# Two-layer attention and FFN kernel: another order of loads and work at the start, gathers tied to chunks, and a written order at the end

## The chip, the cores and the metric

The kernel runs on one core of a Trainium2 chip. The engines are named as the profile names them: PE is TensorE (matmuls and transposes), DVE is VectorE, ACT is ScalarE, POOL is GpSimd, SP is SyncE, which only starts transfers. PEld is PE's loading of weights. The metric is the device time of one execution in microseconds (us); lower is better. Three runs of the kernel before gave 328.57 us in the median, from 328.22 to 328.8.

## The reference

`x` is 2 batches of 1024 rows of 256 numbers, the context is 2 batches of 77 rows of 192. All is float32. Four stages follow one another, each with a residual:

```python
x = x + L0_xattn(layernorm(x), ctx)    # 16 heads of 16, softmax over the 77 context rows
x = x + L0_ffn(layernorm(x))           # relu FFN 256 -> 1024 -> 256; only expert 0 counts; then a layernorm
x = x + L1_xattn(layernorm(x), ctx)    # one head of 256, its own layernorms of x and of the context
x = x + L1_ffn(layernorm(x))           # each position takes one of 8 matrices of 256x256 and one of 8 biases

# L1_ffn
scores = einsum('sp,tp->st', pe, sign(tile_sigs))   # 1024 positions, 8 tiles
idx = argmax(scores, axis=-1)                       # the same for both batches
y_all = einsum('bsd,tod->bsto', x, W) + b
out = take y_all at idx
```

The choice of a matrix depends on the position alone, not on `x`.

## The kernel before

The 2048 rows are cut into 8 chunks of 256 (`NC`), each of two blocks of 128 rows (`NI`); chunks 0 to 3 are batch 0, chunks 4 to 7 batch 1. A chunk goes through `attention0` (with one `attention0_block` per block), `ffn0`, `attention1` and `to_pairs`. All are generators: each `yield` names a place in an abstract order, `begin` puts a generator on a heap, and `run` takes them from the heap by place. So the stages of several chunks are woven into each other: `attention0` of chunk c near place 2c - 2, `ffn0` near 2c + 2.7, `attention1` near 2c + 6. A scheduler below places the instructions on the engines; inside `tc.manual_schedule` an engine keeps the order in which the program wrote them.

For the last stage the 1024 positions are sorted by matrix. `choices` computes scores, the chosen matrix (`oh`), and by counting and triangular sums each row's place in the sorted order (`to`) and its inverse (`who`). Rows of batch 0 are computed in their given order and sent to their sorted places through a DRAM tensor `places` (`to_places`, `from_places`); rows of batch 1 are gathered in sorted order from the start (`rows_of_x`). A sorted batch has 8 blocks of 128 rows; a block can span several matrices, and 15 pairs of a block and a matrix (`NJ`) always cover it. `pairs` computes which block and which matrix each pair has and loads these numbers into registers of ACT, PE and DVE. `pair` copies a block's transposed rows (`nT`, ACT), multiplies them by its matrix (`ps_t`, PE, four matmuls in the trace) and adds the result, scaled by `scale`, to the block's rows `y` (DVE). `scale` is zero for rows that are not the pair's, and otherwise the row's inverse standard deviation. From pair 7 on each pair finishes one block, which POOL scatters to its rows of `out`: eight indirect transfers for each batch.

Because the registers hide which block a pair touches, the program tells the framework which dependences do not hold: `apart` and `apart_of` call `declare_no_dep`. For the scatters, "no row is written twice" takes away the order between them.

Row statistics come from `moments`: two DVE instructions per block, then the inverse root, usually on POOL (an addition and a power). `inverse_root` does it on DVE with twelve small instructions for the second norm of `ffn0` in chunks 6 and 7, and for both later norms of chunk 7.

`beginning` writes the order at the start: six warming matmuls, then `choices`' first step, the context, the keys and chunk 0's rows. The loads stand in front of it. SP starts x of chunk 0, `cols` (all constant columns), `wq`, `wv`, x of chunk 1, `wo`, `rows`; ACT starts the context, `wk`, `sigT` and `peT`. Loads after `late = True` wait until chunk 0's normalised rows have been transposed and copied (`after(loads.pop(), "a0")`).

`PLACES` gives the pairs' places: batch 0 from 18.7 to 21.05, batch 1 from 21.05 to 23.7. Batch 0's pairs so lie between the last chunk's instructions. Gathers keep program order on POOL (`keep_in_program_order`).

Of the kernel before, what the change touches and what calls it, by code (L numbers as in the profile page):

```python
# [37 lines left out]
P = 128  # L38
# [25 lines left out]
def tile_blocks(ctx: ExitStack, tc: tile.TileContext, a: dict, out: bass.AP):  # L64
# [50 lines left out]
    cols = load("cols", [P, N_COL], a["cols"])  # L115
    wq = load("wq", [P, KC, D], rows_of(a["wq"]))
    sigT = load("sigT", [P, NT], a["sigT"], nc.scalar)
    peT = load("peT", [P, S // 4], a["peT"], nc.scalar, tag="hT", bufs=6)
    wv = load_early(1, "wv", CK)
    load_x(1)  # L120
    wo = load("wo", [P, KC, D], rows_of(a["wo"]))

    rows = load("rows", [P, N_ROW, D], a["rows"].partition_broadcast(P))
    late = True
    w1 = load("w1", [P, KC, F], rows_of(a["w1"][0]), tag="w1", bufs=1)
    load_x(2)
    wk1 = load_early(2, "wk1", CK)
# [61 lines left out]
    def moments(x, n, name, p=P, twice=False, vector=False, rs=None, later=False, pin=False):  # L189
        st = work.tile([P, NI, nc.vector.BN_STATS_DIM], F32, tag="st", name=f"st_{name}")  # L190
        mv = work.tile([P, NI, nc.vector.BN_AGGR_DIM], F32, tag="mv", name=f"mv_{name}", bufs=6)
        if rs is None:
            rs = work.tile([P, NI], F32, tag="rs", name=f"rs_{name}", bufs=6)
        for i in range(n):
            ins = nc.vector.bn_stats(st[:p, i, :], x[:p, i, :])  # L195
            if pin:
                tc.keep_in_program_order(ins)
        for i in range(n):
            nc.vector.bn_aggr(mv[:p, i, :], st[:p, i, :])


        eps = EPS * EPS / (1.0 + EPS) if twice else EPS

        def root():
            if vector:
                inverse_root(rs, mv[:, :, 1], eps, name)
            else:
                nc.gpsimd.tensor_scalar(rs[:p, :n], mv[:p, :n, 1], eps, None, ALU.add)
                nc.gpsimd.tensor_tensor(rs[:p, :n], rs[:p, :n], mhalf[:p, :n], ALU.pow)

        if later:
            return mv, rs, root
        root()
        return mv, rs

    def inverse_root(y, v, eps, name):
        w = work.tile([P, NI], F32, tag="w", name=f"w_{name}")
        t = work.tile([P, NI], F32, tag="t", name=f"t_{name}")  # L220
        nc.vector.tensor_scalar(w, v, eps, None, ALU.add)
        yi = y.bitcast(I32)
        nc.vector.tensor_scalar(yi, w.bitcast(I32), 1, None, ALU.logical_shift_right)
        nc.vector.tensor_scalar(yi, yi, -1.0, float(0x5F3759DF), ALU.mult, ALU.add)
        for _ in range(3):
            nc.vector.scalar_tensor_tensor(t, y, -0.5, y, ALU.mult, ALU.mult)
            nc.vector.tensor_tensor(t, t, w, ALU.mult)
            nc.vector.scalar_tensor_tensor(y, t, 1.5, y, ALU.add, ALU.mult)

    def normed(x, n, d, name, m, p=P, out=None, act=False):  # L230
# [10 lines left out]
        for i in range(n):  # L241
            if act:
# [12 lines left out]
    def centred(x, name, mv, act):  # L255
        y = work.tile([P, NI, D], F32, tag="xn", name=f"n_{name}", bufs=4)
        if act:
            sh = work.tile([P, NI], F32, tag="sh", name=f"sh_{name}", bufs=4)
            nc.vector.tensor_scalar(sh, mv[:, :, 0], -1.0, None, ALU.mult)
        for i in range(NI):  # L260
            if act:
                nc.scalar.activation(y[:, i, :], x[:, i, :], AF.Identity, bias=sh[:, i : i + 1])
            else:
                nc.vector.tensor_scalar(y[:, i, :], x[:, i, :], mv[:, i, 0:1], None, ALU.subtract)
# [90 lines left out]
    def masked(e, c, src, eng):  # L355
        mask = cols[:, C_VM + 8 * c : C_VM + 8 * c + 8].unsqueeze(1).unsqueeze(3)
        eng.tensor_tensor(
# [5 lines left out]
    def values():  # L363
# [9 lines left out]
        for c in range(NK):  # L373
# [6 lines left out]
            masked(0, c, ps[:, :D], nc.vector)  # L380
# [8 lines left out]
    def values_by_head():  # L389
        y = work.tile([P, NK, D], F32, tag="ext", name="ext", bufs=1)  # L390
        nc.sync.dma_start(y, v_rows.rearrange("(c p) d -> p c d", p=P))
        for c in range(NK):
            yield
            masked(1, c, y[:, c, :], nc.gpsimd)


    def row_of_biases():
        bvb = work.tile([P, KC, P], F32, tag="oT", name="bvb")
        for k in range(KC):
            nc.vector.tensor_scalar(bvb[:, k, :], ones, col(C_BV + k), None, ALU.mult)  # L400
# [9 lines left out]
    def second_context():  # L410
        m = moments(cx, B, "cx", p=L)
# [62 lines left out]
    def choices():  # L474
        neg = const.tile([P, NT], F32, tag="neg", name="neg")
        sign = const.tile([P, NT], F32, tag="sign", name="sign")
        nc.vector.tensor_scalar(neg, sigT, 0.0, None, ALU.is_lt)
# [156 lines left out]
    def gather(to, src, index):  # L634
        tc.keep_in_program_order(
            nc.gpsimd.indirect_dma_start(
                out=to, out_offset=None, in_=src,
                in_offset=bass.IndirectOffsetOnAxis(ap=index, axis=0),
            )
        )  # L640

    def rows_of_x(c):
        e, s0 = divmod(c * NI, NS)
        for i in range(NI):
            gather(
                xs[c][:, i, :], a["x"].rearrange("b s d -> (b s) d"),
                chosen["who"][:, e, s0 + i : s0 + i + 1],
# [7 lines left out]
    def attention0(c, x):  # L655
        e = c * NI // NS
        m = moments(x, NI, f"a{c}", pin=1 < c < 4)
        yield 2 * c - 1.8
        n = normed(x, NI, D, f"a{c}", m, act=True)
# [11 lines left out]
        for g in range(KC):  # L671
            nc.scalar.activation(qT[:, g, :], ps[:, g, :], AF.Identity, bias=col(C_BQ + g))  # L672
# [72 lines left out]

    def ffn0(c, x):
# [10 lines left out]
        for f in range(0, F // P, 2):  # L757
# [9 lines left out]
            for j in range(2):  # L767
                nc.scalar.activation(  # L768
                    hT[-1][:, j, :], ps[:, j, :], AF.Relu, bias=col(C_B1 + f + j)
                )  # L770
        for i in range(NI):
# [9 lines left out]
        m = moments(tb, NI, f"g{c}", vector=c >= NC - 2)  # L781
# [11 lines left out]
    def attention1(c, x, b):  # L793
        e = c * NI // NS
        keys = slice(e * L, (e + 1) * L)
        last = c == NC - 1
        mv, rs, root = moments(x, NI, f"b{c}", twice=True, vector=last, later=True)
        if not last:
            root()
        yield b + 6.3  # L800
        n = centred(x, f"b{c}", mv, act=not last)
        if last:
            root()
# [49 lines left out]

    def apart(i, others, reason):
        for other in others:
            tc.declare_no_dep(i.ins, other, reason=reason)
# [21 lines left out]
    def apart_of(ins, others, reason):  # L878
        for other in others:
# [258 lines left out]
```

## Time and profile before

The profiled execution took 331.53 us, its span from the first to the last instruction is 329.8 us, and the granted clock of PE was 0.964 in the mean.

| engine | busy us | share of the span | instructions |
|---|---|---|---|
| PE | 289.5 | 88% | 2100 |
| PEld | 241.0 | 73% | 2100 |
| DVE | 206.0 | 62% | 604 |
| ACT | 152.0 | 46% | 331 |
| POOL | 121.5 | 37% | 167 |

The whole span in 40 slices of 8.2 us each, a digit being tenths of busy time (9 is 90% or more), and the clock that PE was granted:

```profile
PE   3997929999969999899899999999995989987690
DVE  1538844947837775594768459468477575675740
PEclk9999987999999999999999999999997899999788
```

In a table by stage, the columns are the stretch in us, its length, the busy time of PE, PEld, DVE, ACT and POOL (with the number of instructions), PE's granted clock, the share of the DMA engines and GB/s. In a row of the order of time, the columns are the start in us, the duration, the engine, the line, the operation, what it writes and reads, and in brackets the idle time before it with what ended it. In a row of the chain of waits they are the start, the time on the chain, and what took it.

### The profile page before, as it was taken

To read this page: it belongs to the slowest core of one execution; us is meant where nothing else is said; L and a number is where in the kernel's file an instruction comes from. 1 tells how busy PE (TensorE), PEld (TensorE's weight loads), DVE (VectorE), ACT (ScalarE), POOL (GpSimd) and SP (SyncE) were. 2 spreads that over 40 slices of the span, in tenths; PEclk is the share of its full clock that TensorE was granted. 3 is DMA by queue.
4 is the path that set the end of the run, shared out by engine and by line. 5 is a ranking of instruction groups with operands and counts; after the bars stand their busy time and mean duration, and the time that the engine had idled before them with its cause. 6 is when DMAs were issued, how large, how long until landed. Compare 5 with 4: busy or idle time off the path is not lost.

```text
span 329.8 us, 5754 instructions
## 1 busy us (share of the span) xinstructions
PE 289.5 (88%) x2100; PEld 241.0 (73%) x2100; DVE 206.0 (62%) x604; ACT 152.0 (46%) x331; POOL 121.5 (37%) x167
## 2 busy tenths in 40 slices
PE   3997929999969999899899999999995989987690
PEld 3865718878858887788688788888885878865470
DVE  1538844947837775594768459468477575675740
ACT  1234427465365455547444663645554464242210
POOL 2210372223271455515454451123175530173153
PEclk9999987999999999999999999999997899999788
DMA  8394210330010001100200100040000000011011
GB/s 221 104 359 134 81 32 0 114 143 3 2 46 4 17 14 43 40 2 17 66 17 5 46 17 2 0 159 2 3 1 0 2 0 0 0 68 64 0 67 64
DMA packets 10456, 16.13 MB, mean 49 GB/s; under 512 B 1186, under 2 KB 7740, under 8 KB 10428
## 3 DMA queue, kind: packets, MB, share of 16 engines
q1 hardware_dynamic: 7847, 10.06, 9.4%
q0 software_dynamic: 1920, 5.25, 5.3%
q10 hardware_dynamic: 661, 0.45, 0.6%
q8 instruction: 17, 0.28, 0.3%
q14 instruction: 11, 0.09, 0.1%
HBM read 11.95 MB, written 3.80 MB: 48 GB/s over the span
## 4 chain that ended last, share of the span: by engine, by line
PE 63%; DVE 18%; POOL 6%; ACT 4%; issue 3%; DMA 3%; DVEq 1%; POOLq 0%; ACTq 0%
PE ps_h L763 14%; PE ps_eo L775 12%; PE ps_t L936 5%; PE ps_pT L721 5%; PE sc L686 4%; PE ps_y L743 3%; PE ps_o L730 3%; PE ps_s L812 3%; PE ps_q L667 3%; DVE pr L697 2%; DVE sm L704 2%; DVE y L941 2%; PE ps_y L838 2%; DMA sigT<-in_sigT 2%; DVE x L789 1%
## 5 line engine op out<-in xcount | busy, mean ns | idle before, releaser
L763 PE MATMUL ps_h<-xT_f,w 128*128 128x256 f32 x256 | 62.3, 386 | 0.2
L775 PE MATMUL ps_eo<-w,hT 128*128 128x256 f32 x256 | 60.4, 391 | 0.0
L775 PEld LDWEIGHTS ps_eo<-w,hT 128*128 128x128 f32 x256 | 49.2, 197 | 6.6 <-DVE st_a L195 0.2
L763 PEld LDWEIGHTS ps_h<-xT_f,w 128*128 128x128 f32 x256 | 46.8, 190 | 8.8 <-issue 2.0
L701 ACT ACTIVATE pr<-pr 128x616 f32<-128x616 f32 x32 | 22.9, 717 | 43.3 <-DVE pr L697 40.3
L695 DVE TENSOR_REDUCE mx<-sc 128x8 f32<-128x616 f32 x32 | 25.2, 788 | 13.4 <-PE sc L686 13.4
L936 PE MATMUL ps_t<-every,nT 128*128 x120 | 31.0, 410 | 2.6 <-DVE y L941 1.3
L768 ACT ACTIVATE hT<-ps_h,cols 128x256 f32<-128x256 f32 x64 | 26.6, 467 | 10.7 <-PE ps_h L763 10.4
L936 PEld LDWEIGHTS ps_t<-every,nT 128*128 128x128 f32 x120 | 24.0, 207 | 7.3 <-ACT nT L930 2.7
L722 ACT COPY pT<-ps_pT 128x512 f32<-128x512 f32 x48 | 25.4, 594 | 5.0 <-PE ps_pT L721 4.9
L653 POOL TENSOR_TENSOR x<-x,rows 128x512 f32<-128x512 f32 x16 | 20.4, 1280 | 19.0 <-DVE rows L404 16.7
L704 DVE TENSOR_REDUCE sm<-pr 128x8 f32<-128x616 f32 x32 | 25.2, 786 | 3.4 <-ACT pr L701 2.5
L743 PE MATMUL ps_y<-wo,oT 128*128 128x256 f32 x64 | 17.9, 404 | 9.3 <-DVE oT L737 9.3
L721 PE MATMUL ps_pT<-ident,pr 128*128 128x128 f32 x160 | 21.4, 279 | 4.7 <-ACT qT L672 2.7
L697 DVE TENSOR_TENSOR pr<-sc,mx 128x616 f32<-128x616 f32 x32 | 25.3, 790 | 0.2
L721 PEld LDWEIGHTS ps_pT<-ident,pr 128*128 128x128 f32 x160 | 18.7, 145 | 6.6 <-ACT qT L672 2.9
L941 DVE SCALAR_TENSOR_TENSOR y<-ps_t,scale,y 128x256 f32 x30 | 14.4, 479 | 11.5 <-PE ps_t L936 8.7
L947 POOL DMA_INDIRECT out<-y,who x16 | 16.0, 1000 | 14.1 <-DVE y L941 7.7
L842 DVE SCALAR_TENSOR_TENSOR x<-ps_y,sm,x 128x256 f32<-128x256 f32 x16 | 7.0, 479 | 21.8 <-PE ps_y L838 21.8
L743 PEld LDWEIGHTS ps_y<-wo,oT 128*128 128x128 f32 x64 | 11.9, 198 | 11.7 <-DVE oT L737 10.3
L930 ACT COPY nT<-nT 128x256 f32 x30 | 11.4, 405 | 19.0 <-PE ps_t L936 17.7
L730 PE MATMUL ps_o<-pT,vbd 128*32 128x128 f32 x512 | 17.9, 277 | 0.0
(204 smaller groups left out, 498.5 us busy)
## 6 DMA issues: line engine op xcount, KB each, us to landing
w<-in_w SPq DMA_DIRECT2D x2, 1024.0 KB, 10.1
every<-in_wrow SPq DMA_DIRECT2D x1, 2048.0 KB, 9.3
x<-in_x SPq DMA_DIRECT2D x4, 256.0 KB, 4.6
y<-places SPq DMA_DIRECT2D x4, 256.0 KB, 4.5
rows<-in_rows SPq DMA_DIRECT2D x1, 640.0 KB, 4.9
ext<-v_rows SPq DMA_DIRECT2D x1, 640.0 KB, 4.4
v_rows<-v SPq DMA_DIRECT2D x1, 616.0 KB
early<-in_wv SPq DMA_DIRECT2D x2, 192.0 KB, 5.9
```

The source lines that it names most:

```text
L695: nc.vector.tensor_reduce(mx, scv, AX.X, ALU.max)
L697: nc.vector.tensor_tensor(p8.rearrange("p (j h l) -> p j h l", j=4, l=L), scv, mx.unsqueeze(3).to_broadcast([P, 4, 2, L]), ALU.subtract,)
L701: nc.scalar.activation(p8, p8, AF.Exp, scale=1.0 / math.sqrt(HD))
L704: nc.vector.tensor_reduce(sm[:, g * 8 : g * 8 + 8], pr[:, g, :G8].rearrange("p (h l) -> p h l", l=L), AX.X, ALU.add,)
L721: nc.tensor.transpose(ps[:, j * P : (j + 1) * P], srcs[4 * n + j], ident)
L722: nc.scalar.copy(pT[:, n].rearrange("p j t -> p (j t)"), ps)
L730: nc.tensor.matmul(ps[32 * m : 32 * m + 32, g * P : (g + 1) * P], vbd[:, e, n, g, 32 * m : 32 * m + 32], pTs[:, g * NK + n, :], start=n == ...
L743: nc.tensor.matmul(ps[:, :D], oT[:, g, :], wo[:, g, :], start=g == 0, stop=g == KC - 1)
L763: nc.tensor.matmul(ps[:, j, :], w1[:, k, (f + j) * P : (f + j + 1) * P], tT[:, k, :], start=k == 0, stop=k == KC - 1,)
L768: nc.scalar.activation(hT[-1][:, j, :], ps[:, j, :], AF.Relu, bias=col(C_B1 + f + j))
L775: nc.tensor.matmul(ps[:, :D], hT[f // 2][:, f % 2, i * P : (i + 1) * P], w2[:, f, :], start=f == 0, stop=f == F // P - 1,)
L936: nc.tensor.matmul(ps, nT[:, k * P : (k + 1) * P], late_weights["every"][:, bass.ds(t + k * D, D)], start=k == 0, stop=k == KC - 1,)
```

## The change

At the start, `cols` is loaded in two parts (the 30 columns in front of `C_RANK` first), `wv` moves to ACT's queue in front of `sigT` and `peT`, x of chunk 1 moves up, and of `rows` only the first row is loaded early. `choices` and `second_context` leave `beginning` and begin at places 1.55 and 1.6; their first instructions, and the statistics of chunk 1, wait for chunk 0's queries (`"q0"`). Chunk 0's second block is normalised on DVE. Two of the five mask products of the first values move to POOL behind an ACT copy.

A gather no longer keeps program order; it waits for a given chunk's transposed FFN input (`"f0"` and so on). The mask products of batch 1 wait for `"f0"`.

`inverse_root` is gone: all roots are on POOL. Batch 0's pairs get places 16.7 to 18.6. `run` stops at place 18.7, and what is left of chunk 6's second attention and of its `to_pairs`, the second half of the last chunk's FFN, its second attention, its `to_pairs` and batch 1's pairs are written out in `ending`, in a manual order on PE, DVE, ACT and POOL, the last chunk block by block. `apart_of` now keeps a dependence when both instructions are in the ending and are issued by the same engine.

```diff
-    cols = load("cols", [P, N_COL], a["cols"])
+    cols = const.tile([P, N_COL], F32, tag="cols", name="cols")
+    nc.sync.dma_start(cols[:, :C_RANK], a["cols"][:, :C_RANK])
     wq = load("wq", [P, KC, D], rows_of(a["wq"]))
+    wv = load_early(1, "wv", CK, nc.scalar)
+    load_x(1)
+    nc.sync.dma_start(cols[:, C_RANK:], a["cols"][:, C_RANK:])
+    wo = load("wo", [P, KC, D], rows_of(a["wo"]))
...
+            if c < 3:
+                masked(0, c, ps[:, :D], nc.vector)
+            else:
+                copied = work.tile([P, NI, D], F32, tag="xn", name=f"v_{c}", bufs=4)[:, 0, :]
+                nc.scalar.copy(copied, ps[:, :D])
+                masked(0, c, copied, nc.gpsimd)
...
-            masked(1, c, y[:, c, :], nc.gpsimd)
+            after(masked(1, c, y[:, c, :], nc.gpsimd).ins, "f0")
...
-    def gather(to, src, index):
-        tc.keep_in_program_order(
-            nc.gpsimd.indirect_dma_start(
...
+    def gather(to, src, index, behind):
+        i = nc.gpsimd.indirect_dma_start(
+            out=to, out_offset=None, in_=src,
+            in_offset=bass.IndirectOffsetOnAxis(ap=index, axis=0),
+        )
+        after(i.ins, behind)
...
+    in_end = {}
+
+    def apart_of(ins, others, reason):
+        for other in others:
+            if not (ending_now and in_end.get(other.name) == ins.engine):
+                tc.declare_no_dep(ins, other, reason=reason)
+        if ending_now:
+            in_end[ins.name] = ins.engine
...
     def beginning():
-        sort, context, inner, vals = choices(), first_context(), second_context(), values()
-        a0, a1 = attention0(0, xs[0]), attention0(1, xs[1])
-        warm(6)
-        next(sort)
+        context, vals, a0 = first_context(), values(), attention0(0, xs[0])
+        warm(8)
         next(context)
         next(a0)
-        warm(2)
+        warm(3)
         next(context)
         next(a0)
+        next(context, None)
+        warm(3)
         next(a0)
+        warm(2)
         next(a0)
...
+    def ending(att, h):
...
+        def stats(k, i, rows):
+            nc.vector.bn_stats(st[k][i], rows)
+            nc.vector.bn_aggr(mv[k][i], st[k][i])
+            root(rs[k][i], mv[k][i][:, 1:2], k == "b")
...
+        def fill(p):
+            pair_nT(e, p)
+            pair_mm(e, p)
+
+        ending_now.append(True)
+        next(att)
+        fill(0)
+        next(att, None)
+        next(h)
+        pair_add(e, 0)
+        eo(0)
+        g_stats(0)
+        next(h)
+        eo(1)
+        g_scaled(0)
+        g_added(0)
+        next(h, None)
+        turn(0)
+        g_stats(1)
+        fill(1)
+        score(0)
+        g_scaled(1)
+        softmax(0)
+        fill(2)
+        g_added(1)
+        weights(0)
+        pair_add(e, 1)
+        valued(0)
+        turn(1)
+        h_stats(0)
+        fill(3)
+        score(1)
+        h_turn(0)
+        softmax(1)
+        pair_add(e, 2)
+        fill(4)
+        weights(1)
+        pair_add(e, 3)
+        scales(e, range(NS - NI, NS - 1), NS - 1)
+        valued(1)
+        fill(NS - NI)
+        h_stats(1)
+        pair_add(e, 4)
+        fill(5)
+        h_turn(1)
+        scales(e, range(NS - 1, NJ), NS)
+        pair_add(e, NS - NI)
+        pair_add(e, 5)
+        for p in range(NS - 1, NJ):
+            fill(p)
+            pair_add(e, p)
...
-    PLACES = (
-        [18.7] * 4 + [19.55] * 8 + [21.05] * 3,
-        [21.05] + [21.85] * 3 + [21.97] * 2 + [22.9 + 0.1 * p for p in range(9)],
-    )
-    for e in range(B):
-        for p in range(NJ):
-            begin(PLACES[e][p], pair(e, p, PLACES[e][p]))
-    run(math.inf)
+    for p in range(NJ):
+        place = 16.7 + 0.25 * p if p < 6 else 18.2 + 0.05 * (p - 6)
+        begin(place, pair(0, p, place))
+    run(END)
+    with tc.manual_schedule(engines=on_all):
+        ending(att, h)
```

`fill(p)` is pair p's copy and product, `pair_add(e, p)` its addition and, from pair 7 on, the scatter. `eo` is the FFN's second product of a block; `g_`, `turn`, `score`, `softmax`, `weights`, `valued` and `h_` are one block's steps of the norm behind it, of the second attention and of `to_pairs`.

## The prediction

> **What bounds the kernel now.** I read the 40 slices first, then busy time by stage, then the chain of waits, then the order of time where PE (TensorE) has holes.
>
> ```profile
> 0.00:14.00 14.00, 8.49 (x48) 7.77 (x48) 3.94 (x19) 3.17 (x7) 3.23 (x18) 1.00 0.61 181
> 14.00:37.00 23.00, 20.59 (x145) 15.51 (x145) 15.69 (x48) 8.42 (x19) 4.20 (x6) 1.00 0.57 182
> 37.00:50.00 13.00, 6.13 (x73) 4.56 (x73) 7.40 (x18) 4.83 (x10) 7.19 (x11) 0.87 0.23 72
> 90.00:235.00 145.00, 139.42 (x1133) 117.24 (x1132) 96.62 (x248) 77.72 (x165) 59.28 (x75) 1.00 0.10 28
> 300.00:312.00 12.00, 6.50 (x27) 4.62 (x26) 8.46 (x34) 3.32 (x9) 1.81 (x2) 0.90 0.05 17
> 312.00:330.00 18.00, 9.50 (x34) 7.58 (x33) 4.36 (x9) 2.03 (x5) 7.80 (x8) 0.78 0.17 60
> ```
>
> The second figure is PE's busy time. From 90 to 235 us PE works 139 of 145 us: nothing is to be had there, and the change leaves that order nearly alone. The holes are at both ends, where the change works. At the start, the chain and the order of time show three of them:
>
> ```profile
> 1.75 5.12 DMA sigT<-in_sigT
> 14.41 3.78 PE ps_q L667 x8
> 37.37 4.38 DMA ext<-v_rows
> 45.97 0.75 POOL rs_a L209
> 46.75 1.15 DVE L238 SCALAR_TENSOR_TENSOR sh_a<-mv_a,rs_a 128x2 f32<-128x2 f32 x1 [4.22 <-POOL rs_a L209]
> 49.70 2.07 PE L743 MATMUL ps_y<-wo,oT 128*128 128x256 f32 x4 [6.58 <-DVE oT L737]
> ```
>
> DVE (VectorE) starts with a sorting instruction that waits for sigT until 6.89, and the first rows' statistics queue behind it. The first query product takes 3.78 us where the same eight matmuls take 1.89 later. Near 42 us POOL (GpSimd) multiplies masks on `ext`, issues two gathers, and only then takes chunk 2's root; DVE waits 4.22 us for it, PE 6.58. At the end:
>
> ```profile
> 252.38 1.96 PE L812 MATMUL ps_s<-wqkg,xT_b 128*128 128x77 f32 x8 [3.61 <-DVE tb L779]
> 310.67 10.83 PE L936 MATMUL ps_t<-every,nT 128*128 x36 [1.11 <-ACT nT L930]
> 315.25 0.99 POOL L947 DMA_INDIRECT out<-y,who  x1 [6.64 <-DVE y L941]
> 323.34 0.97 POOL L947 DMA_INDIRECT out<-y,who  x1 [0.30 <-issue]
> 324.62 0.97 POOL L947 DMA_INDIRECT out<-y,who  x1 [0.30 <-issue]
> ```
>
> The last eight scatters sit on POOL at 1.28 us each (0.97 and 0.30 of issue), seven steps and two waits from 315.25 to 324.62; 5.2 us of landing and closing follow. The span is 329.8, the profiled execution 331.53, the median of the runs 328.57: I sum in the span, add 1.7 and scale by 328.57/331.53.
>
> **The start.** x of chunk 0 has landed by 4.55 (the load that reuses its semaphore issues then without waiting), against statistics at 7.18: 2.6 us. Its second half is normed on DVE (0.34 for such a subtraction) beside ACT's (0.59): 0.5 saved. Statistics 0.74 + 0.30, POOL's root 1.3, shift 0.16, norm 0.6 put the rows at about 7.8 instead of 11.4. PE must first run 8 + 3 + 3 warm matmuls, the context transposes and the keys. ACT's fifth load now waits for the context's landing (4.05), so its table load (1.28) ends near 6.3 instead of 4.0 and the first ACT copy comes no sooner.
>
> What PE then costs depends on its clock. The row: in the present run PE worked nearly without a hole from 8.17, and matmuls turned fast only near 19.3, 11 us later. [...] At present PE warms 2.93 us and then idles 4; the change fills 1.15 to 13 nearly whole. [...]
>
> Then scores run at once and the first maximum starts near 16 (19 to 20 by the row) instead of 23.23. In block 1 the 3.1 us of DVE sorting (30.37 to 33.5) is gone too, and two mask products of 0.41 move to POOL behind ACT copies, unneeded until `ps_o`.
>
> For chunk 2 POOL's order is now root first, with masks and gathers behind f0: of DVE's 4.22 us about 1.0 stays (root 0.22 + 0.72), and `sh_a` should not take 1.15 again. What is late next is PE itself: it is full from 50 to 90, and the moved sorting (`ps_who` 1.70, counts, places and their warming, about 4 us) lands there. Counted at 48 us I am 11.8 ahead; less 4 of sorting, plus about 1 of half clock (50 to 53.7) that no longer happens: **8.5 us**, from 3 to 12. Masks (5 x 0.6) and gathers (2 x 1.2) now stand ahead of chunk 3's root on POOL and delay it some 1.4 us; DVE has 3.7 us of idleness before its next maximum (71.47), which hides it. Without that it costs the 1.4. The later gathers wait for ACT copies that POOL's preceding addition nearly implies: nothing.
>
> **The end, up to the last chunk's FFN.** Batch 0's pairs move ahead of it: 14 pairs and one of batch 1, 0.86 each on PE, with chunk 6's last products (2.0), 14.8 us. In the hole at 248.8, DVE's addition waited behind two scale products held by POOL; then PE ran at half clock to 258 (eo took 5.74 instead of 3.6). In the new order two pairs fill part of it, and eo of chunk 6 ends near 255.6 instead of 259.9 with 1.7 of pairs done: 6.0 back. I allow 3 for new stalls (this stage shows one of 0.9). The last chunk's first eo ends at 276.5 + 14.8 - 6.0 + 3 = 288.3.
>
> **The last chunk by blocks.** Four DVE roots (12 small instructions, 2.4 us, stretched to 7.0 for g) become POOL pairs at 1.2. Along the written order from that eo: add, statistics, root, two products, centring 3.75; transposes, copy, and pair 1, which is queued ahead of the scores, 6.9; softmax and pair 2 ahead of the weights' transpose 9.5; values, statistics 11.9; block 1 the same, held by pairs 3 and 4, to its centring at 17.9; transpose, copies, pair 7 and its addition 20.7. First scatter: 309.0, 6.2 us before the present 315.25. Batch 0's eight scatters (10.2 us of POOL) now precede the roots; by my count they end over 3 us before the first is due. Had they no such cover, they would delay the chain one for one.
>
> **The scatters.** The new `apart_of` keeps a dependence inside the ending if both instructions are issued by the same engine. For POOL's arithmetic that is free; the scatters are DMAs. In the built order each of batch 1's scatters, from the second on, waits for its predecessor's semaphore as well as its own lane's. Nothing but later scatters is queued behind, but the end waits for them. The row for a completed scatter of this shape:
>
> ```profile
> 215.17 0.97 POOL L865 DMA_INDIRECT places<-x,to  x1 [0.30 <-issue]
> 217.59 1.90 SPq L876 DMA_DIRECT2D y<-places  x4
> ```
>
> SP reads `places` on completion: 2.42 from the start, plus 0.28 of issue: 2.7 a step. [...] I take 18.9 (17 to 22): it replaces the 9.37 between first and last scatter, **+9.5**.
>
> **Sum.** -8.5 - 6.2 + 9.5 = -5.2: span 324.6, profiled 326.3, median **323.4**.
>
> **Rivals.** (a) *Scatters still flow* (12%): the wait is met before the next issue. For it: data move within 2 us of a start; against: 2.42 to SP. 9.5 less: 314.
> (b) *PE's clock falls in the ending* (20%), slower: fillers are gone and holes of about 1 us stand between its products. Present drops follow idleness of 2.5 us and more (at 46.9, 251.5, 309.5); 44% busy at 301 to 305 caused none, so mostly against. Some 8.3 us of matmuls lie on the path from the second eo to the first scatter; at half clock they double: 331.6. It decides once over 5.2 us of them run slow.
> (c) *The start gives most back* (10%): clock by the row and PE full from 50 on, gain 3: 328.9.
> (d) *A completion takes 4 us* (8%), under eight returning writes: 7 x 1.3 more, 332.4.
>
> **Numbers.** The forecast has 50%, its own range 319 to 328. For 8 in 10 I reach from between (a) and it to (b): 315.5 to 332. A measurement of this kernel tells 0.2% (0.7 us) from no change. Faster: nearly all of the forecast, (a), and a share of (b) to (d) that is half as bad: 0.68; same 0.06; slower 0.26.
>
> **What would show it.** First maximum near 16; no hole of 6 us near 45; the eight last scatters 2.7 apart rather than 1.28; first scatter near 300 on the new clock of time; PEclk full between eo and it. I am wrong if the maximum stays at 20 or later, if steps are 1.3 or 4, or if PEclk drops in the ending.

## The result, and the profile after

The changed kernel takes **354.82 us** (median of 4 runs, 353.57 to 356.83) beside 328.64 us for the kernel before (4 runs, 328.22 to 328.80): a ratio of **1.0805, 95% interval 1.0752 to 1.0857**. It is slower by 26 us, where 323.4 was forecast. In later groups of runs both kernels show shorter and longer runs (346.3 to 347.2 and 355.4 to 356.0 us; 322.4 to 325.8 and 329.8 to 331.4 us), and the ratios below are of the shorter ones; like compared with like, the change costs 7 to 8 percent. The profiled execution took 353.57 us, with a span of 351.8.

First the page of the changed kernel: two rows of the 40 slices (8.8 us each), and one row of the groups (busy time and mean ns of one, then POOL's idle time before it and what ended most of that).

```profile
PE   8889897999399969979997999998998978678400
...
PEclk9969999899789999999999999999999999957955
...
L627 POOL DMA_INDIRECT bias<-in_b,tid x8 | 9.2, 1151 | 28.6 <-ACT xT_f L272 27.7
```

Between 80 and 240 us, where PE had one slice under 8 before (a 6), it now has a 3 at 88 to 97 us, a 6 at 123 to 132, and a 7 at 150 and at 185. The clock row falls to 5 and 7 at 308 to 325. The third row is a group that does not appear on the page of the kernel before: gathers, with 28.6 us of POOL's idle time in front of them, 27.7 of it ended by an ACT copy of `xT_f`.

Busy time by stage (length, then busy time and count of PE, PEld, DVE, ACT and POOL, the granted clock, the DMA share and GB/s):

```profile
0.00:14.00 14.00, 12.62 (x80) 11.35 (x80) 4.34 (x19) 4.37 (x9) 3.34 (x19) 1.00 0.75 220
14.00:37.00 23.00, 20.68 (x181) 14.76 (x173) 16.17 (x43) 10.94 (x23) 6.37 (x10) 0.85 0.53 160
37.00:50.00 13.00, 12.22 (x120) 10.64 (x121) 11.70 (x30) 7.60 (x18) 4.79 (x5) 1.00 0.02 4
...
90.00:235.00 145.00, 131.47 (x1052) 110.61 (x1053) 89.52 (x233) 75.22 (x158) 55.55 (x72) 0.98 0.09 25
296.00:308.00 12.00, 9.08 (x43) 7.09 (x42) 7.50 (x25) 2.90 (x8) 5.67 (x10) 0.97 0.00 1
308.00:324.00 16.00, 12.73 (x38) 9.29 (x37) 7.82 (x23) 4.59 (x14) 3.27 (x6) 0.60 0.00 1
```

The first and third rows are better than before: PE works 12.62 of the first 14 us (it was 8.49) and 12.22 of the 13 from 37 to 50 (it was 6.13). The stage from 90 to 235, of which the prediction said that nothing was to be had there, falls from 139.42 to 131.47. In the last row the granted clock is 0.60. The second row has a loss too: its clock is 0.85, where it was 1.00. (The trace's record of the clock begins at 6.87 us here and at 19.39 in the kernel before. Ahead of that the column says 1.00 for want of a record.)

Now the order of time, in three places (start, duration, engine, line, operation, and in brackets the idle time of that engine and what ended it):

```profile
15.56 0.76 DVE L687 TENSOR_REDUCE mx<-sc 128x8 f32<-128x616 f32 x1
...
84.75 1.09 POOL L627 DMA_INDIRECT bias<-in_b,tid  x1 [5.95 <-ACT xT_f L272]
86.14 0.95 POOL L627 DMA_INDIRECT x<-in_x,who  x1 [0.30 <-issue]
87.13 0.23 POOL L217 TENSOR_SCALAR rs_g<-mv_g 128x2 f32<-128x2 f32 x1
87.52 1.00 POOL L627 DMA_INDIRECT x<-in_x,who  x1 [0.16 <-issue]
88.55 0.74 POOL L218 TENSOR_TENSOR rs_g<-rs_g,mhalf 128x2 f32<-128x2 f32 x1
...
89.32 0.88 DVE L786 SCALAR_TENSOR_TENSOR x<-tb,rs_g,x 128x256 f32<-128x256 f32 x2 [3.84 <-POOL rs_g L218]
...
89.46 1.25 POOL L627 DMA_INDIRECT bias<-in_b,tid  x1 [0.17 <-issue]
90.75 0.24 POOL L217 TENSOR_SCALAR rs_a<-mv_a 128x2 f32<-128x2 f32 x1
...
94.71 1.54 PE L713 MATMUL ps_pT<-ident,pr 128*128 128x128 f32 x6 [6.11 <-ACT qT L663]
...
324.21 1.10 POOL L963 DMA_INDIRECT out<-y,who  x1 [3.57 <-DVE y L955]
327.51 0.97 POOL L963 DMA_INDIRECT out<-y,who  x1 [2.21 <-DVE y L955]
...
346.66 0.97 POOL L963 DMA_INDIRECT out<-y,who  x1 [2.29 <-DMA out<-y,who]
```

The first maximum on DVE starts at 15.56 (23.23 before). At 84.75 POOL begins a gather, then one more; only then the first half of the root `rs_g`, a third gather, the second half of the root, a fourth gather, and the root `rs_a`. Each gather holds POOL for 1.0 to 1.3 us. The same happens at the roots of the next three chunks, with four, four and two gathers. DVE stands 3.84 us for `rs_g` and PE 6.11 us for what follows from `rs_a`. At the end, the eight scatters of batch 1 come 3.2 us apart, each after 2.2 to 2.3 us in which POOL is idle.

The span can be cut at four points: where POOL starts the root of chunk 7's FFN moments, where DVE adds the last chunk's first `eo`, and where the first and the last of batch 1's scatters start. The columns on the right are kernels that are described below. The forecast is the prediction's, on the new kernel's clock of time.

| stage, us | before | forecast | after | after again (`e5_after`) | both losses undone (`e3_both`) | before again (`e9_before`) |
|---|---|---|---|---|---|---|
| start to chunk 7's FFN root | 248.7 | 240.2 | 255.5 | 256.5 | 242.6 | 245.4 |
| to the first `eo` addition | 27.8 | 39.6 | 41.6 | 39.0 | 39.0 | 27.7 |
| to the first scatter of batch 1 | 38.7 | 20.7 | 27.1 | 22.3 | 22.3 | 36.5 |
| first to last scatter | 9.4 | 18.9 | 22.5 | 22.4 | 9.0 | 9.0 |
| to the end of the span | 5.1 | 5.2 | 5.1 | 5.1 | 5.1 | 5.1 |
| span | 329.8 | 324.6 | 351.8 | 345.4 | 318.1 | 323.7 |

Of the 27.2 us between forecast and span, 15.3 stand in the first row, 2.0 in the second, 6.4 in the third and 3.6 in the fourth. The start was won at chunk 0, and by chunk 7 more than that was lost again.

### The profile page after: what moved, and what is told of

It reads as the page before. It is cut to its first block, busy times and chain, and to the rows that moved or that the text cites. A ratio compares the mean times of both kernels' runs of the same rounds, so it can differ in the third digit from the quotient of the medians.

```text
span 351.8 us, 5767 instructions
## 1 busy us (share of the span) xinstructions
PE 294.4 (84%) x2116; PEld 243.7 (69%) x2116; DVE 200.3 (57%) x561; ACT 152.8 (43%) x336; POOL 129.7 (37%) x184
## 5 line engine op out<-in xcount | busy, mean ns | idle before, releaser
L757 PE MATMUL ps_h<-xT_f,w 128*128 128x256 f32 x256 | 64.4, 396 | 4.6 <-ACT hT L762 4.6
L757 PEld LDWEIGHTS ps_h<-xT_f,w 128*128 128x128 f32 x256 | 48.6, 197 | 14.0 <-ACT hT L762 6.0
L772 PE MATMUL ps_eo<-w,hT 128*128 128x256 f32 x224 | 51.0, 381 | 0.0
L772 PEld LDWEIGHTS ps_eo<-w,hT 128*128 128x128 f32 x224 | 41.5, 190 | 5.3 <-DVE st_a L203 0.2
L947 PE MATMUL ps_t<-every,nT 128*128 x120 | 33.0, 421 | 10.0 <-ACT nT L938 10.0
L713 PE MATMUL ps_pT<-ident,pr 128*128 128x128 f32 x160 | 23.4, 288 | 13.9 <-ACT qT L663 6.1
L947 PEld LDWEIGHTS ps_t<-every,nT 128*128 128x128 f32 x120 | 23.8, 209 | 15.4 <-ACT nT L938 12.1
L762 ACT ACTIVATE hT<-ps_h,cols 128x256 f32<-128x256 f32 x64 | 26.6, 468 | 12.5 <-PE ps_h L757 12.1
L955 DVE SCALAR_TENSOR_TENSOR y<-ps_t,scale,y 128x256 f32 x30 | 14.5, 482 | 13.4 <-PE ps_t L947 9.6
L233 ACT ACTIVATE n_a<-x,sh_a,rs_a 128x256 f32<-128x256 f32 x15 | 8.5, 601 | 27.1 <-DVE sh_a L228 27.1
L627 POOL DMA_INDIRECT bias<-in_b,tid x8 | 9.2, 1151 | 28.6 <-ACT xT_f L272 27.7
L722 PE MATMUL ps_o<-pT,vbd 128*32 128x128 f32 x512 | 18.9, 281 | 0.0
L217 POOL TENSOR_SCALAR rs_f<-mv_f 128x2 f32<-128x2 f32 x8 | 1.8, 220 | 45.6 <-DVE mv_f L209 45.6
```

The source lines that it names most:

```text
L713: nc.tensor.transpose(ps[:, j * P : (j + 1) * P], srcs[4 * n + j], ident)
L722: nc.tensor.matmul(ps[32 * m : 32 * m + 32, g * P : (g + 1) * P], vbd[:, e, n, g, 32 * m : 32 * m + 32], pTs[:, g * NK + n, :], start=n == ...
L757: nc.tensor.matmul(ps[:, j, :], w1[:, k, (f + j) * P : (f + j + 1) * P], tT[:, k, :], start=k == 0, stop=k == KC - 1,)
L762: nc.scalar.activation(hT[-1][:, j, :], ps[:, j, :], AF.Relu, bias=col(C_B1 + f + j))
L772: nc.tensor.matmul(ps[:, :D], hT[f // 2][:, f % 2, i * P : (i + 1) * P], w2[:, f, :], start=f == 0, stop=f == F // P - 1,)
L947: nc.tensor.matmul(ps, nT[:, k * P : (k + 1) * P], late_weights["every"][:, bass.ds(t + k * D, D)], start=k == 0, stop=k == KC - 1,)
```

## The experiments

The theory behind them is a ledger of three losses that do not depend on one another: gathers ahead of the roots, serial scatters, and half clock in the ending. The rivals are given with each.

### One loss undone at a time

`e1_flow`, scatters apart again:

```diff
-            apart(i, groups, "no row is written twice")
+            for other in groups:
+                tc.declare_no_dep(i.ins, other, reason="no row is written twice")
```

> The changed kernel, with the eight scatters of batch 1 declared apart from one another again; all else is as changed. Ledger theory (three separate losses: gathers ahead of the roots about 12 us, a longer and half-clocked ending about 7 us behind the last chunk's first sum, serial scatters about 13 us): the first scatter starts where it did, near 324, the seven behind it follow 1.28 us apart as in the kernel before (9 us instead of 22.4), the time falls by about 13 us to 341 to 342. Rival: a scatter waits for its own rows too (the pair additions come 0.87 us apart, less than a scatter), or the writes of the scatters themselves take the 2.3 us: then the starts stay about 3.2 us apart and the time stays at 354.

Measured: 332.99 us, ratio to the kernel before 1.026 (1.013 to 1.039). Two of its scatters:

```profile
318.58 0.97 POOL L963 DMA_INDIRECT out<-y,who  x1 [0.30 <-DVE y L955]
...
326.25 0.97 POOL L963 DMA_INDIRECT out<-y,who  x1 [0.31 <-issue]
```

They are 1.28 us apart again, 0.30 of it idle; first to last takes 9.1 us. The rest of the gain, beyond the 13 us forecast, is not the edit's: in this execution the ending kept full clock (1.00 from 294 to 322 us), which the first profile of the changed kernel did not (0.60 from 308 to 324). The control below (`e5_after`, 345.4 in the span) with full clock stands 14.0 above this span of 331.4.

`e2_gathers`, gathers as before, and `e3_both`, both edits:

```diff
-        after(i.ins, behind)
+        tc.keep_in_program_order(i)
```

> The changed kernel, with the gathers placed as before (kept in written order, no wait for a given chunk); scatters still in series. Ledger theory: the gathers' waits move three or four gathers of 1.0 to 1.3 us each on POOL right ahead of the roots of chunks 0 to 4, so the roots come 4 to 5 us late and TensorE stands idle; without them the root of the FFN's first moments of chunk 7 comes about 11.6 us earlier (255.5 to about 244), and the time falls by 10 to 13 us to 342 to 345. Rival: POOL is simply loaded more (masks of batch 0's values and all roots on it), and the gathers stand ahead of the roots wherever they are put: within 3 us of the changed kernel, 352 to 355.

> Both edits: the scatters of batch 1 apart, the gathers as before; the new loads and start and the written ending stay. Ledger theory: the two losses add, 354.8 - 13 - 11.5 = about 330 (327 to 333), so no faster than the kernel before (328.6): the written ending gives back what the start wins. Rival (the start is worth 8.5 us and the ending costs nothing beyond the scatters): 316 to 321.

Measured: `e2_gathers` 334.23 us, ratio 1.026 (1.008 to 1.044); `e3_both` 320.70 us, ratio 0.986 (0.967 to 1.004), so not told from the kernel before by these runs. All three expectations missed by the same cause: they counted from 354.8, whose ending ran at half clock, and these profiles kept full clock there. So `e3_both` fell below the 327 to 333 of its theory and into the range of its rival. Repeated with more runs as `e11_both_again`, it is told from the kernel before.

> Both losses undone, once more, as the control for the filled ending and for the kernel before on one chip: 317.8 to 321.5 at full clock in the ending, about 325 at half clock, ratio to the kernel before 0.98 to 0.99.

Measured: 320.34 us, ratio 0.988 (0.981 to 0.995). So the two losses add. In spans, of profiles that all kept full clock in the ending (pairs 1 to 4 take 1.13 us each for their four products), the control has 345.4; the scatters alone give back 14.0, the gathers alone 13.4, both 27.3. The root of chunk 7's FFN comes at 242.55 in `e3_both` and at 255.82 in `e1_flow`: 13.3 us for the gathers. In order of time, `e3_both` at the place shown above, and two of its pair products in the ending:

```profile
85.23 0.51 POOL L217 TENSOR_SCALAR rs_g<-mv_g 128x2 f32<-128x2 f32 x1 [6.17 <-DVE mv_a L209]
85.82 0.71 POOL L218 TENSOR_TENSOR rs_g<-rs_g,mhalf 128x2 f32<-128x2 f32 x1
...
86.56 0.88 DVE L786 SCALAR_TENSOR_TENSOR x<-tb,rs_g,x 128x256 f32<-128x256 f32 x2 [0.90 <-POOL rs_g L218]
...
87.62 0.22 POOL L217 TENSOR_SCALAR rs_a<-mv_a 128x2 f32<-128x2 f32 x1 [1.10 <-DVE mv_a L209]
...
88.81 1.09 POOL L627 DMA_INDIRECT bias<-in_b,tid  x1 [0.17 <-issue]
...
91.19 1.08 POOL L627 DMA_INDIRECT x<-in_x,who  x1 [0.19 <-issue]
...
289.96 1.13 PE L947 MATMUL ps_t<-every,nT 128*128 x4 [1.70 <-ACT nT L938]
...
296.38 1.13 PE L947 MATMUL ps_t<-every,nT 128*128 x4 [1.40 <-ACT nT L938]
```

Both halves of `rs_g` stand together now, `rs_a` follows once DVE has delivered its input, and the gathers come behind them. DVE waits 0.90 us for the first and 0.41 for the second, where it stood 3.84 for `rs_g` alone.

### The gathers: the wait, or the place?

`e4_before_waits` puts only the new gathers, with their waits, into the kernel before (the same edit of `gather`, `rows_of_x` and the bias gathers as in the change).

> The kernel before with one part of the change alone: each gather waits for the ACT copy of a given chunk, as in the changed kernel. Ledger theory: the same bunches of gathers stand ahead of the roots of chunks 1 to 4, so 8 to 12 us are lost: 337 to 341. Rival (a gather's wait is nearly implied by the order and costs nothing, as the prediction took it): 328 to 330.

Measured: 346.16 us, ratio 1.064 (1.050 to 1.078). That is some 20 us more than the kernel before, and more than the 8 to 12 expected. First what PE waited for in the changed kernel from 75 to 200 us, then the same view of `e4_before_waits` from 75 to 220, and last `e3_both` from 75 to 200 (total us, times, longest):

```profile
PE ps_pT L713 <- ACT qT L663: 6.1, 1, 6.1
PE ps_h L757 <- ACT hT L762: 4.6, 3, 1.6
PE ps_pT L713 <- DVE x L736: 4.2, 3, 1.7
```

```profile
PE ps_pT L720 <- ACT qT L671: 6.1, 1, 6.1
PE ps_h L762 <- ACT hT L767: 4.6, 3, 1.6
PE ps_pT L720 <- DVE x L743: 4.2, 3, 1.7
```

```profile
PE ps_pT L713 <- ACT qT L663: 2.7, 1, 2.7
```

The holes of the first two are the same to a tenth, 14.9 us; with both losses undone 2.7 are left. What is more in `e4_before_waits` is the clock. In its profile, which is of its longest run (351.51 us), the clock was 0.86 to 0.95 over these four chunks, and PE was busy 119.1 us; the changed kernel had 1.00 over the last three of them, and 111.3 us. That the clock made the rest of the 20 us is likely from this, but it was not tried apart.

`e7_wait_in_order` has both the wait and the written order of before, with the scatters apart.

```diff
+        tc.keep_in_program_order(i)
         after(i.ins, behind)
```

> The changed kernel with the scatters apart, and the gathers with both their waits for given chunks and the written order of before. This tells the wait from the place that it gave the gathers in POOL's row. Theory (the wait itself is met by the time that POOL gets there; the loss comes from the gathers standing ahead of the roots): within 0.5 percent of the kernel with both undone, 317 to 322. Rival (the wait itself costs, by its semaphore or by holding POOL until the copy): 4 us or more above it, 325 to 333.

Measured: 320.43 us, ratio 0.990 (0.981 to 0.998), as with both undone. Its root of chunk 7's FFN comes at 242.33. So the wait as such showed no cost here. In order of time, and with two pair products of its ending:

```profile
86.62 0.51 POOL L217 TENSOR_SCALAR rs_g<-mv_g 128x2 f32<-128x2 f32 x1 [6.16 <-DVE mv_a L209]
...
89.01 0.22 POOL L217 TENSOR_SCALAR rs_a<-mv_a 128x2 f32<-128x2 f32 x1 [1.10 <-DVE mv_a L209]
...
90.19 1.09 POOL L627 DMA_INDIRECT bias<-in_b,tid  x1 [0.17 <-issue]
...
289.74 2.07 PE L948 MATMUL ps_t<-every,nT 128*128 x4 [1.70 <-ACT nT L939]
...
299.25 2.08 PE L948 MATMUL ps_t<-every,nT 128*128 x4 [1.19 <-ACT nT L939]
```

The roots `rs_g` and `rs_a` stand ahead of the gather, as in `e3_both`. What cost the time is the gathers' place: in the changed kernel they start when the copy that they wait for ends (`<-ACT xT_f` at 84.75), which is just where the roots fall due. No run took away the written order without adding the wait, so it is not shown which of the two moved them.

### The ending, and the clock

> The changed kernel itself once more, as the control for the other kernels of this call on their chip. Its first profile showed half clock in the ending (27.3 us from the last chunk's first sum to its first scatter, where the three experiments with one part undone took 18.9) and an ACT copy 3.0 us late at 290.85. Theory that both belong to the execution and not to the order: here 18.9 us again, a span of 341 to 345, ratio 1.04 to 1.06. Rival, that the late gathers and the serial scatters together keep the clock down: above 27 us and over 350 again.

The control's four times were 346.27, 347.17, 355.36 and 355.95 us, and the profile is of the faster pair; its ending is the one in the table. (In the expectation 27.3 us was counted from the first `eo`, but 18.9 from the second; counted as in the table it is 22.3.) So half clock in the ending (0.50 from 307.2 to 320.9 us in the first profile) belongs to some executions of the same program, and costs 5 to 6 us behind the first `eo`: 27.1 us in the first profile and 28.6 in `e7_wait_in_order`, beside 22.3. The two pair products shown of `e7_wait_in_order` take 2.07 and 2.08 us; the same ones in `e3_both` 1.13. The copy that came 3.0 us late at 290.85 in the first profile, and makes the second row of the table 41.6 instead of 39.0, was in no other profile of these kernels; what held it stays open.

`e10_held` fills the holes, with both losses undone. The bank that the fillers write is taken from the pairs, in an edit not shown here:

```diff
...
-        def fill(p):
+        held = late_banks[1].tile([P, 512], F32, tag="held", name="held")
+
+        def hold(n):
+            for _ in range(n):
+                nc.tensor.matmul(held[:, :P], ones, ones, start=True, stop=True)
+
+        def fill(p, n=0):
             pair_nT(e, p)
+            hold(n)
             pair_mm(e, p)
...
-        fill(1)
+        fill(1, 4)
...
-        fill(2)
+        fill(2, 9)
...
+        hold(2)
         valued(0)
...
-        fill(3)
+        fill(3, 4)
...
-        fill(4)
+        fill(4, 7)
...
+        hold(2)
         valued(1)
...
-            fill(p)
+            fill(p, 5 if p == NS - 1 else 0)
```

> Both losses undone, and the holes of TensorE in the written ending (0.8, 1.7, 0.4, 0.8, 1.4, 0.4 and 1.0 us) filled with 33 products of ones that no one reads, with one bank less for the pairs. TensorE is 49 to 65 percent busy in the 8 us behind the last chunk's first sum, and in some executions the clock then falls to half for the rest of the ending, which costs 6 to 8 us. Theory (the low share decides it): with the holes filled the ending keeps full clock in every run, all within 2 us of 318 to 321, where the unfilled one spread over 317.8 to 326. Rival (the fillers stand in the way, or the clock falls for another reason): slower than 322, or the same spread.

Measured: 320.38 us, ratio 0.990 (0.985 to 0.995), six times from 319.7 to 321.7. Its first scatter comes 22.4 us behind the first `eo`: the fillers cost nothing on the path. The unfilled ending beside it gave 317.75 to 325.32. Of the 19 runs of the four unfilled kernels with both losses undone (`e3_both`, `e7_wait_in_order`, `e8_later_rows`, `e11_both_again`), seven stand 5 us or more above the shortest of their kernel; of the 12 with fillers (this one and `e12_masks` below) none stands more than 4 us above. That supports the theory; with so few runs it does not prove it.

### The start

> The kernel before with the changed loads and beginning alone (its own gathers, roots, places of the pairs and ending). From the profile with both losses undone, whose chunk 7 reaches the root of its FFN moments at 242.55 against 248.74 before: a gain of 5 to 7 us, ratio about 0.98. The prediction's 8.5 us would give 0.974. Rival (the sorting, moved on, gives the start back): 0.995 to 1.005.

`e6_start` is the kernel before with the changed loads, `beginning`, masks of values, the waits for "q0" and the new places of the sorting; its gathers, roots, pairs and ending are those of before. Measured: 322.96 us, ratio 0.9985 (0.9956 to 1.0014): not told from no change, as its rival had it. Its span was 319.1 in the profile, which is of its fastest run, with chunk 7's FFN root at 240.3.

> The kernel before itself, for its trace on this chip, since it ran at 322.5 at its best beside the earlier experiments and at 328.6 beside the changed kernel. Two readings of the start alone, which came out only 0.2 percent faster than the kernel before: (1) the kernel before loses less at its start on this chip than in the first profile (its 6.6 us hole of TensorE ahead of ps_y at 43 to 50, or the wait for sigT), so that chunk 7's FFN root, at 248.7 in the first profile, comes at 241 to 244 here, and the start is worth 1 to 3 us; (2) its root comes at 246 to 249 here too, the start is worth 6 to 8 us, and they are lost in the ending.

Measured: 327.84 us, in a group of runs from 322.4 to 331.1 for this kernel. In its profile chunk 7's root comes at 245.39, between the two readings that were expected. Its start is that of the first profile. The largest row of PE's waits in its first 60 us (total us, times, longest):

```profile
PE ps_y L743 <- DVE oT L737: 6.6, 1, 6.6
```

That is the hole of 6.6 us that the prediction showed, so the first reading's cause is not it. The 3.3 us that separate the two profiles of the kernel before come almost wholly at chunks 3 and 4, 1.6 us each. In the first profile PE waits 1.4 us for `oT` in each of them and in `e9_before` it does not; the cause stays open. Against `e9_before`, the start is worth 2.8 us at chunk 7 in `e3_both`, 5.1 in `e6_start` and 5.0 in `e11_both_again`. These are differences of single profiles: that of `e9_before` is of a run 3 us above the shortest of its kernel, that of `e6_start` of the shortest of its 12. By all runs of `e6_start`, the start alone is worth at most 0.4 percent, 1.4 us.

The new start also has a stretch of half clock, which is the 0.85 of the second row by stage. In the first profile of the changed kernel the clock is 0.50 from 20.5 to 27.4 us, for 6.8 us. In `e3_both` it is 0.66 in the mean from 20 to 30 us, also 6.8 us of half clock; in `e6_start` 0.92 from 10 to 20 and 0.91 from 20 to 30, together 3.4 us; in `e12_masks` it is still 0.93 from 30 to 40. The root of chunk 0's FFN comes at 41.50, 41.65, 39.19 and 43.91 us in these four: earliest behind the shortest stretch, latest where there is half clock beyond 30 us. In the other seven profiles with the new start it comes between 39.5 us (`e11_both_again`) and 42.8. The two profiles of the kernel before have no half clock from 19.4 to 46.5 us. The 5.1 and 5.0 above are from the two profiles whose chunk 0 is earliest.

Where did the rest of the 8.5 go? In the first profiles of both, the changed kernel is 12.1 us ahead at the root of chunk 0's FFN (41.50, before 53.58), but at chunk 1's only 4.5 (73.90, before 78.42). Chunk 3's root has its input at 55.0 and starts at 59.0, behind five masks and two gathers; PE then has a hole of 2.9 us. Two edits went for it, both on top of both losses undone. `e8_later_rows`:

```diff
-            begin(2 * c - 3.5, once(rows_of_x, c))
+            begin(2 * c - 3.5 + (0.8 if c == NC // B else 0), once(rows_of_x, c))
```

> Both losses undone, and the first two row gathers (chunk 4, at 56.7 and 58.2) placed 0.8 later, behind the row addition of chunk 1's FFN instead of ahead of chunk 3's root. There they hold the root from about 56.5 to 59.1, and TensorE stands 2.8 us at 59 to 62 and then runs at half clock. Theory (the same mechanism once more): the chunks behind come 2.5 to 4 us earlier, 314 to 317. Rival (the root waits for the masks' transfer at 53.5 anyway): as with both undone, 317 to 321.

Measured: 326.9 us (321.41 to 327.31), no gain: its one run near 321 is no faster than the 319.9 to 320.4 of `e7_wait_in_order` beside it. In order of time:

```profile
70.95 0.22 POOL L217 TENSOR_SCALAR rs_f<-mv_f 128x2 f32<-128x2 f32 x1 [9.82 <-DVE mv_f L209]
...
76.03 1.22 POOL L627 DMA_INDIRECT x<-in_x,who  x1 [0.18 <-issue]
...
79.06 0.43 DVE L203 BATCH_NORM_STATS2 st_a<-x 128x6 f32<-128x256 f32 x1 [4.08 <-DMA x<-in_x,who]
...
92.16 1.54 PE L713 MATMUL ps_pT<-ident,pr 128*128 128x128 f32 x6 [4.17 <-ACT qT L663]
```

Chunk 1's root comes 28.3 us behind chunk 0's, where it is 32.4 to 32.7 in the others, as meant, and PE's hole at 59 to 62 is gone. But the gather, now at 76.03, makes DVE wait 4.08 us for chunk 4's rows, and what stands behind that statistics instruction on DVE waits too: `mv_g`, whose statistics end at 74.98, starts at 80.11. PE's hole before 92.16 grows from 2.7 us (`e3_both`) to 4.17, and chunk 2's root comes at 105.09, later than the 103.74 of `e3_both`. In this profile the ending ran at half clock as well (0.50 from 294 to 306 us): of the 7.4 us by which its span exceeds that of `e3_both`, 6.0 stand there. The expectation was right about the root and wrong about the sum.

`e12_masks`, with both losses undone and the filled ending as well, moves the masks instead:

```diff
-            after(masked(1, c, y[:, c, :], nc.gpsimd).ins, "f0")
+            after(masked(1, c, y[:, c, :], nc.gpsimd).ins, "a3")
...
-    begin(3.5, paced(3.5, 0.4, values_by_head()))
+    def in_places(gen, places):
+        for _, place in zip(gen, places):
+            yield place
+
+    begin(3.5, in_places(values_by_head(), [4.62 + 0.02 * k for k in range(20)]))
```

> Both losses undone and the ending filled, as before, and one more edit at the start: the five masks of batch 1's values (3.0 us of POOL, at 53.5 to 56.5) are made behind chunk 3's root instead of ahead of it, which also puts the first two row gathers behind that root. The root of chunk 3, at 59.1 in the profile with both losses undone though its input is there at 55.0, comes at about 55.3, TensorE's hole of 2.8 us at 59 to 62 and the half clock behind it go, and the root of chunk 1's FFN moments comes 28.5 to 30 us behind chunk 0's instead of 32.5. Unlike the later gathers alone, chunk 4's rows land by 61, long before their statistics are due. Theory: the gain stays to the end, 315 to 318, ratio 0.975 to 0.985. Rival (the gain is given back at chunk 2, as with the later gathers): 319 to 322, ratio 0.985 to 0.995.

Measured: **317.43 us** (314.29 to 318.16), ratio **0.978 (0.971 to 0.985)**: the fastest of all, and faster than both kernels. In order of time:

```profile
57.49 0.22 POOL L217 TENSOR_SCALAR rs_a<-mv_a 128x2 f32<-128x2 f32 x1 [8.51 <-DVE mv_a L209]
...
58.69 1.22 POOL L627 DMA_INDIRECT x<-in_x,who  x1 [0.19 <-issue]
...
71.87 2.41 POOL L343 TENSOR_TENSOR vbd<-ext,cols 128x256 f32<-128x256 f32 x4 [9.39 <-ACT xT_a L272]
```

The root goes first, then the gathers, and four of the five masks fill POOL's idle time at 72; the fifth stands between the two halves of chunk 1's root. The root of chunk 1's FFN follows chunk 0's by 30.3 us instead of 32.7 in `e10_held`, and chunk 2's follows by 27.6, so nothing is given back.

## Why the prediction was wrong, point by point

**"The later gathers wait for ACT copies that POOL's preceding addition nearly implies: nothing."** This step failed, and it alone would have turned the sign. The clause on the wait is right (`e7_wait_in_order`); what it left out is that the edit also took away the written order. Two to four gathers of 0.9 to 1.3 us then stood ahead of or between two roots, in four chunks. For the scatters the prediction had asked what is queued behind the waiting instruction; for the gathers it asked only how long the wait is, and not what POOL then works through. The periods between FFN roots are 33.5, 31.2, 31.2 and 30.4 us in the changed kernel for chunks 1 to 5, and 29.6, 27.8, 27.8 and 27.8 in `e3_both`: 13 us where nothing was forecast. "From 90 to 235 ... the change leaves that order nearly alone" falls with it.

**The scatters.** The mechanism was right: serial, and only inside the ending. The step was mis-sized: the 18.9 is seven steps of 2.7 us, and 3.2 were measured, 3.6 us more over seven. In the chain of waits of the changed kernel (start, duration, what):

```profile
340.22 0.97 DMA out<-y,who
...
343.39 2.41 DMA out<-y,who
```

A scatter lands 2.41 us after its start, which is what the row of before had (2.42). But the next one starts at 346.66, 0.86 us behind that landing, while the prediction added 0.28 of issue. So the mis-sized term is this restart; what fills it stays open.

**The start.** That products turn fast early enough for a first maximum "near 16", from which the 8.5 is counted, no run had shown: by the row of before it would have been 19 to 20. The changed kernel showed it: the record of full clock begins at 6.87 us, 5.7 behind the first product (19.39 and 18.2 before), the first query products take 1.99 us at 9.74 (3.78 before), the first maximum comes at 15.56, and chunk 0's root 12.1 us ahead. The 8.5 was too much. Two terms failed: the "1.4" for masks and gathers ahead of chunk 3's root, which are 4.0 us, and that DVE's idleness hides them; PE stood 2.9 us. Moving the masks gave 2.4 us back at chunk 1. A third was missing: the half clock at the start, from 20.5 us on in the first profile. Between `e6_start`, with 3.4 us of it, and `e12_masks`, where it passes 30 us, chunk 0's root moves by 4.7 us. The 4 us put down for the sorting were not tried apart.

**The end up to the last FFN** was right in its sum: 39.6 us forecast, 39.0 in every profile of the written ending but the first. Its terms (6.0 won, 3 for new stalls) were not tried apart. **The last chunk by blocks** was 20.7 forecast and is 22.3 at full clock, 27 to 29 at half clock.

**Rivals.** (a), scatters that flow, did not come. (b), half clock in the ending, did come in the first profile and in some runs of others; "holes of about 1 us" and up to 1.7 between products went with it, and the argument that present drops (at 46.7, 251.5 and 309.5 us) follow idleness of 2.5 us and more was too strong. (c), the start giving most back, came in size (its gain of 3 us beside 2.8 to 5.1 by profiles and at most 1.4 by the runs of `e6_start`) but not for its reason, as the record of full clock begins at 6.87 us already. (d), 4 us a completion, did not come. No rival named the gathers, so the range, to 332, could not hold 354.8.

## What to carry to other kernels

A wait that is met in time can still cost, since it may move the waiting instruction to another place in its engine's row: after such an edit, read the row around every short instruction on the critical path (here roots of 0.9 us behind gathers of 0.9 to 1.3), not the wait. When a written order is replaced by dependences, price the two apart. The order between the scatters cost the landing and the restart behind it at every step, 2.41 and 0.86 us here; before an order is forced on stores that touch different rows, multiply such a step by their number.

## What was not expected of the hardware

The clock fell in an ending without a long hole. In `e7_wait_in_order` no hole of PE behind the first `eo` was over 1.7 us, and PE was busy 9.08 of 12 us from 281 to 293; from 289.7 on four products of a pair took 2.07 us instead of 1.13, and the granted clock from 293 to 310 was 0.59. `e3_both`, with the same holes (0.8, 1.7, 0.8 and 1.4 us) and 8.56 of 12 us at full clock, kept 1.00 from 280 to 308.

The traces show what goes with it. In the first profiles of both kernels every change of the clock is a whole multiple of 3.41 us behind the one ahead of it, as on a grid of steps. In the changed kernel the record begins at 6.87 us, and the clock changes at 20.52, 27.35, 61.48, 64.90, 92.20, 99.03, 307.24, 320.89 and 334.55: 4, 2, 10, 1, 8, 2, 61, 4 and 4 steps. In the kernel before it begins at 19.39, and the changes are at 46.70, 53.52, 251.50, 258.32, 309.52, 316.35 and 326.59: 8, 2, 58, 2, 15, 2 and 3 steps. In the endings of `e7_wait_in_order` and `e8_later_rows` half clock lasts 17.0 us, five steps (from 289.8 and from 291.6).

Eight profiles have the unfilled written ending. In the three where the clock fell (the first one, `e7_wait_in_order`, `e8_later_rows`), the step just ahead of the fall begins 6.8, 5.0 and 5.2 us behind the first `eo`, and PE is busy for 42, 45 and 50 percent of it. Of the five that kept full clock, `e3_both` and `e1_flow` have a later change (at 311.0 and 324.8 us, the products done) from which the steps can be counted back: the emptiest in the 20 us behind the first `eo` begins 5.6 and 6.1 us behind it, and PE is busy for 50 percent of it in both. So the steps lie at another place of the program in each of these five executions, and the same holes fall into one step in some and are shared between two in others. The share does not decide it alone: 50 percent stands on both sides, and in the first profile a step of 44 percent, from 286.8 us on, was followed by no fall. No run moved the grid, so the cause is not proven.
